# A two-layer network on one core: statistics' roots on VectorE, value maps ahead of the small maps, constants loaded over later slots

## The chip, the core and the metric

The kernel runs on one core of a Trainium2 chip. A core has five engines, each with its own queue of instructions: TensorE (PE in the profile, with its weight loads as PEld), VectorE (DVE), ScalarE (ACT), GpSimd (POOL) and SyncE (SP), which only issues transfers here. PSUM is the memory into which TensorE writes and from which VectorE and ScalarE read. Instructions of one engine run in their program order, and engines wait for each other through semaphores. The metric is the device time of one execution in microseconds (us); the time of the kernel before is the median of three runs.

## The reference, cut to what matters

The input x is 8 images of 256 channels by 64 by 64 pixels in float32. Two layers follow one another, each with a group norm ahead of it and a residual sum.

```python
x = x + L0(gn(x)); x = x + L1(gn(x))       # gn: 32 groups, (g - mean) / sqrt(var + 1e-5)

def L0(x):                                 # a conv whose weights are made from x
    x1, x2, x3 = conv1x1(x, w1, b1), conv1x1(x, w2, b2), conv1x1(x, w3, b3)   # 32, 32, 256 channels
    h = concat([x1, unfold3x3(reflect_pad(x2))])
    h = conv1x1(relu(bn1(h)), cw1)
    w = conv1x1(relu(bn2(h)), cw2, cb2)    # 9 weights for each of 32 groups
    return sum over the 9 taps of unfold3x3(pad(x3)) * w

def L1(x):
    q, k, v = three 1x1 convs of 256 channels, 4 heads
    att = softmax of q . (k + position) over a 7x7 window; out_att = att . v
    wts = softmax over 9 taps of conv1x1(x, Wfc)       # 9 x 256 channels
    oc = depthwise3x3(relu(depthwise3x3(x, w1_tap)), w2_tap), for each tap
    return rate1 * out_att + rate2 * sum over taps of oc * wts
```

`bn` is a batch norm with given statistics, which also takes `1 / sqrt(var + 1e-5)`.

## The kernel before

An image is cut into 8 bands of 8 rows (512 pixels), and the 256 channels into two halves of 128 partitions. Layer 0 runs 12 bands (`AHEAD`) ahead of layer 1. The outer loop counts g from -12 to 63: slots g < 0 hold layer 0 alone (the prologue, `alone` in the code); from g = 0 on, a slot holds band g of layer 1 and beside it band g + 12 of layer 0. A slot has 8 steps, each with six calls of `advance()`, so 48 to a slot. The order of the instructions is written out by hand: `beside(g, s)` gives what is issued in step s at its head, middle and end, and `after(n, f)` puts f behind the n-th `advance()` from now. Nothing reorders instructions afterwards; each engine gets its own in the order in which the program issues them.

Layer 0 of a band runs over three slots. In the first, `small_maps` makes x1 and x2 on TensorE (L328), and `write_maps` writes them with their bias by eight ScalarE instructions (L343) into three shifted copies; GpSimd fills the borders. `value_maps` makes x3 for each half (L369), ScalarE adds the bias (L374), and the result is stored to DRAM (L376), by ScalarE's queue in the prologue. In the prologue the small maps stand in step 0 and the value maps in steps 2 and 3; in the main loop the value maps stand at the end of step 0 and in step 1. In the second slot `hidden_maps` makes the hidden channels on ScalarE (L418) and TensorE (L428); `values_by_group` and `x_by_group` have SP load x3 and x in another layout (x3q, xg). In the third, `tap_weights` makes the nine weights on TensorE (pw, L464), VectorE multiplies them with the shifted values (prod, L477), and GpSimd adds six products into xg (L485). In the prologue the other three products are added up by TensorE (sco_sum, L498), VectorE combines both (L505), and `keep` stores the band by four transfers on ScalarE's queue (L523).

The group norm's statistics of an image are handled by `gn_affine`: group means by a small product pg (L237), their copies and differences gm and d (L246 to L250), a second product, then `sc = 1 / sqrt(pg + eps)` and `bi` (L269). Chain a (`scaled_weights`) belongs to layer 0 and goes on into scaled weights and a product pb (L304); chain b (`norm_rows`) belongs to layer 1 and goes on into a product pgc (L542). Chain a of image 0 stands ahead of all slots and that of image 1 in the prologue; those of images 2 to 7 lie in the main loop, in band 3 of an image. Chain b of images 1 to 7 lies in the main loop, in band 6. Their products take one of the four PSUM buffers of the tag "gen", which pq, pk, pf, pw, p3 and the transposed probabilities use too.

In layer 1 the scores (sco, L736) are the product of queries and kb, the keys with position, which VectorE finishes (L700, L707) right ahead of them. A score tile of two banks serves two steps. VectorE masks the scores and takes their minimum (L750), ScalarE takes the exponentials (L758), VectorE the reciprocal of their sums (L765), ScalarE scales (L767), TensorE transposes (ptp, L773), and the weighted values follow (small, L785). The branch of Wfc is the products pf (L872), ScalarE's exponentials (L877) and GpSimd's sums; VectorE runs the depthwise convolutions (acc, L829 and L855).

Of the kernel before, what the change touches and what calls it, by code (L numbers as in the profile page):

```python
# [9 lines left out]

F32 = mybir.dt.float32
BF16 = mybir.dt.bfloat16
AF = mybir.ActivationFunctionType
ALU = mybir.AluOpType
AX = mybir.AxisListType
# [3 lines left out]
P = 128  # L19
# [36 lines left out]
CHUNK = R * KW  # L56
NPROB = 2 * CHUNK
NEG = -1.0e30


AHEAD = NB + 4
# [25 lines left out]
def conv_layers_kernel(ctx: ExitStack, tc: tile.TileContext, ins: dict, out: bass.AP):  # L87
# [14 lines left out]
        return t  # L102


    late = []

    def load(name, shape, src=None, now=True):
        t = const.tile(shape, F32, name=f"c_{name}")
        late.append(lambda: nc.scalar.dma_start(out=t, in_=ins[name] if src is None else src))
        if now:  # L110
            late.pop()()
        return t

    gmat = load("gmat", [P, P])
# [13 lines left out]
    wfc = load("wfc", [P, NCT, KK - 1, C], wfc_in[:, :, : KK - 1], now=False)  # L128

    ident = const.tile([P, P], F32, name="ident")  # L130
    make_identity(nc, ident)
# [8 lines left out]
    for t in probs + x3n + h2n:  # L140
        nc.gpsimd.memset(t, 0.0)

    def rstd_(out_, var, eps):
        nc.vector.tensor_scalar(out_, var, eps, None, ALU.add)
        nc.scalar.activation(out_, out_, AF.Sqrt)
        nc.vector.reciprocal(out_, out_)


    bn1s = const.tile([P, 3], F32, name="bn1s")
    bn1b = const.tile([P, 3], F32, name="bn1b")  # L150
    bn2s = const.tile([P, 1], F32, name="bn2s")
    bn2b = const.tile([P, 1], F32, name="bn2b")
    for s, t, g, b_, m, v, n, p in (
        (bn1s, bn1b, PG, PB, PM, PV, 3, P),
        (bn2s, bn2b, PG2, PB2, PM2, PV2, 1, P),
    ):
        rstd_(s, par[:p, v : v + n], BN_EPS)
# [28 lines left out]
    def layer1_loads():  # L186


        last = w1.tile([P, NCT, 1, C], F32, tag="oc", name="last")
        for f in late:  # L190
            f()
        nc.scalar.dma_start(out=last, in_=wfc_in[:, :, KK - 1 :])

        def first():
            nc.vector.tensor_scalar(wv, wv, rate1, None, ALU.mult)

        def difference(kt):
            nc.vector.tensor_sub(wfc[:, kt], wfc[:, kt], last[:, kt].to_broadcast([P, KK - 1, C]))  # L200

        return [first, lambda: difference(0), lambda: difference(1)]

    class Image:
        def __init__(self):
# [9 lines left out]
    def after(n, f):  # L215
        later.append((place[0] + n, f))

    def advance():
# [3 lines left out]
        for f in ready:  # L222
            f()

    def gn_affine(sts, means, name, done):
# [7 lines left out]
        gm, d, sc, bi = (stat.tile([P, n], F32, name=f"{v}_{name}", tag=f"{v}{n}") for v in ("gm", "d", "sc", "bi"))  # L233

        def group_means(v, k):
            pg = ps.tile([P, n], F32, name=f"pg_{name}_{k}", tag="gen", bufs=4)
            nc.tensor.matmul(pg, means, v, start=True, stop=True)  # L237
            return pg


        def a1():
            pg = group_means(mean, 0)
            after(2, lambda: a2(pg))

        def a2(pg):
            nc.vector.tensor_copy(gm, pg)  # L246
            for ct in range(n):
                c = slice(ct, ct + 1)
                nc.vector.tensor_scalar(d[:, c], pg[:, c], mean[:, c], None, ALU.subtract)
                nc.vector.tensor_scalar(d[:, c], d[:, c], d[:, c], var[:, c], ALU.mult, ALU.add)  # L250
            after(5, a3)

        def a3():
            pg = group_means(d, 1)
            after(2, lambda: a4(pg))

        def a4(pg):
            nc.vector.tensor_scalar(sc, pg, GN_EPS, None, ALU.add)
            after(2, a5)

        def a5():
            nc.scalar.activation(sc, sc, AF.Sqrt)
            after(4, a6)

        def a6():
            nc.vector.reciprocal(sc, sc)
            for ct in range(n):
                c = slice(ct, ct + 1)
                nc.vector.tensor_scalar(bi[:, c], gm[:, c], sc[:, c], -1.0, ALU.mult, ALU.mult)  # L269
            done(sc, bi)  # L270

        after(3, a1)


# [13 lines left out]
    def scaled_weights(b):  # L288

        im = images[b]  # L290

        def scale(sc, bi):
            im.w12s = w0.tile([P, NCT, 2 * REL], F32, tag="w12s", name=f"w12s_{b}", bufs=1)
            im.w3s = w0.tile([P, NCT, C], F32, tag="w3s", name=f"w3s_{b}", bufs=1)
            for kt in range(NCT):
                nc.scalar.activation(im.w12s[:, kt], w12[:, kt], AF.Copy, scale=sc[:, kt : kt + 1])
                nc.scalar.activation(im.w3s[:, kt], w3[:, kt], AF.Copy, scale=sc[:, kt : kt + 1])
            after(5, lambda: through(bi))

        def through(bi):  # L300
            pb = ps.tile([P, 1 + NCT], F32, tag="gen", name=f"pb_{b}", bufs=4)
# [6 lines left out]
            after(2, lambda: biases(pb))  # L308
# [26 lines left out]
    def write_maps(b, i, p12):  # L335
        im = images[b]
        t = im.x2[i] = w0.tile([P, HR, W], F32, tag="x2", name=f"x2_{b}_{i}", bufs=2)
        bias = im.bias
        for u in range(2):
            r, o = u * R // 2, 64 * u  # L340
            for q, (dst, src) in enumerate(((1, 0), (0, 0), (0, 1))):
                n = W - (q != 1)
                nc.scalar.activation(  # L343
                    t[32 * q : 32 * q + 32, r + 1 : r + 1 + R // 2, dst : dst + n],
                    p12[o : o + 32, :, src : src + n], AF.Identity, bias=bias[o : o + 32, 0:1],
                )
            nc.scalar.activation(
                t[96:128, r : r + R // 2, :], p12[o + 32 : o + 64], AF.Identity, bias=bias[o + 32 : o + 64, 0:1]
            )
# [179 lines left out]
    def norm_rows(b):  # L529
        im = images[b]  # L530


        def keep(sc, bi):
            both = stat.tile([P, 2], F32, name=f"both_{b}", tag="both")
            nc.vector.tensor_copy(both[:, 0:1], sc)
            nc.vector.tensor_copy(both[:, 1:2], bi)
            after(3, lambda: by_channel(both))

        def by_channel(both):
            pg = ps.tile([P, NCT, 2], F32, tag="gen", name=f"pgc_{b}", bufs=4)  # L540
            for ct in range(NCT):
                nc.tensor.matmul(pg[:, ct], gc[:, ct], both, start=True, stop=True)  # L542
            after(2, lambda: take(pg))
# [369 lines left out]
    def beside(g, s):  # L913
# [48 lines left out]
        alone = g < 0  # L962
        if 0 <= g + AHEAD < B * NB:
            bq_, iq = divmod(g + AHEAD, NB)
            if alone and s == 0:
                mid.append(lambda: small_maps(bq_, iq, small_tile(f"{bq_}_{iq}"))())
            if s == (2 if alone else 0):
                (mid if alone else end).append(lambda: value_maps(bq_, iq, 0, alone))
            if s == (3 if alone else 1):
                mid.append(lambda: value_maps(bq_, iq, 1, alone))  # L970
        if 0 <= g + AHEAD - 1 < B * NB and s == (2 if alone else 1):
            bh, ih = divmod(g + AHEAD - 1, NB)
# [37 lines left out]
    with tc.manual_schedule():  # L1010
# [14 lines left out]
        scaled_weights(0)  # L1025
        for _ in range(32):
            advance()
        for n, f in enumerate(layer1_loads()):
            after(4 * STEPS * (3 + n), f)

        pending, before, conv, convs = [], None, None, []
        for g in range(-AHEAD, B * NB):
            b, i = divmod(g, NB)
            for s in range(STEPS):
# [156 lines left out]
```

## Time and profile before

| what | us |
|---|---|
| median of three runs (3908.52 to 3914.09) | 3910.43 |
| the profiled execution | 3911.49 |
| its span | 3909.7 |
| PE busy in it | 3778.1 |
| DVE, POOL, ACT busy | 3419.7, 3172.5, 2835.8 |
| first score matmul (end of the prologue) | 235.0 |
| first, second and third combination of a band (L505) | 68.86, 87.42, 103.78 |
| the two differences of Wfc on VectorE | start at 56.57 and 72.53 |
| issue and landing of the first x3q | 42.36, 50.22 |

The profile comes from one execution. Its span runs from the first to the last instruction; 1.8 us of the execution lie around it. Busy time of an engine counts the time in which it has an instruction under way; a share of 97% for PE is a mean over the prologue and the main loop. In a row of an engine's timeline the columns are the start, the duration, the engine, the line, the operation, and what it writes and reads; a bracket gives the idle time ahead of it and the engine and tile that ended it.

### The profile page before, as it was taken

What the parts mean: (1) busy time and instruction counts of PE and PEld (TensorE: products, weight loads), DVE (VectorE), ACT (ScalarE), POOL (GpSimd) and SP (SyncE); (2) the same over time, 40 slices, a digit from 0 to 9 for tenths busy, and PEclk for the clock granted to TensorE, in tenths of its full rate; (3) what the DMA queues carried; (4) which work ended last, traced back from release to release, by engine and by line L of the source; (5) the groups of instructions that cost most, each with busy time, mean ns of one, the idle gap of its engine ahead of it and who ended that gap; (6) DMA issues with size and microseconds to landing.
All of it is one profiled execution on the core that took longest, in us unless ns stands there. A gap on an engine that the chain in (4) does not pass through costs nothing.

```text
span 3909.7 us, 71679 instructions
## 1 busy us (share of the span) xinstructions
PE 3778.1 (97%) x24620; PEld 2112.2 (54%) x24620; DVE 3419.7 (87%) x7143; ACT 2835.8 (73%) x6779; POOL 3172.5 (81%) x2156
## 2 busy tenths in 40 slices
PE   5889999999999999999999999999999999999998
PEld 2445555555555555555555555555555555555554
DVE  6879898899898999899998998989988889978778
ACT  4457777777777777777777777777777777677776
POOL 4768888888887988888888888978988888956665
PEclk9999999999999999999999999999999999999999
DMA  8764443543444543543444443444433443322221
GB/s 245 208 168 128 127 118 115 143 121 116 124 123 123 142 118 105 140 131 114 139 111 128 136 119 113 127 138 116 130 111 100 133 122 94 87 85 79 72 60 35
DMA packets 429710, 473.36 MB, mean 121 GB/s; under 512 B 60992, under 2 KB 322208, under 8 KB 429088
## 3 DMA queue, kind: packets, MB, share of 16 engines
q1 hardware_dynamic: 412768, 453.01, 41.1%
q10 hardware_dynamic: 16576, 15.76, 1.3%
q8 instruction: 194, 3.18, 0.3%
q14 instruction: 172, 1.41, 0.1%
HBM read 329.08 MB, written 143.00 MB: 121 GB/s over the span
## 4 chain that ended last, share of the span: by engine, by line
PE 41%; DVE 24%; POOL 15%; ACT 11%; issue 6%; DMA 3%; SPq 0%; ACTq 0%; POOLq 0%; DVEq 0%
PE pf L872 19%; POOL xg L485 8%; DVE prod L477 7%; DVE acc L855 5%; DVE rec L893 5%; POOL ex L1087 4%; PE small L785 3%; PE pv L594 3%; ACT x L343 3%; PE ptp L773 3%; PE sco L736 3%; PE pk L692 2%; PE pq L670 2%; ACT ex L877 2%; DMA x<-x3n 2%
## 5 line engine op out<-in xcount | busy, mean ns | idle before, releaser
L872 PE MATMUL pf<-yp,c_wfc 128*128 128x512 f32 x4096 | 1916.6, 594 | 17.8 <-ACT ex L877 6.8
L485 POOL TENSOR_TENSOR xg<-xg,prod 128x1024 f32<-128x1024 f32 x549 | 1198.8, 2184 | 106.7 <-DVE prod L477 82.5
L872 PEld LDWEIGHTS pf<-yp,c_wfc 128*128 128x128 f32 x4096 | 738.5, 190 | 719.0 <-issue 629.2
L1087 POOL TENSOR_TENSOR ex<-ex,ex 128x1024 f32<-128x1024 f32 x384 | 908.2, 2365 | 66.4 <-ACT ex L877 62.5
L829 DVE SCALAR_TENSOR_TENSOR acc<-yp,c_chan,acc 128x504 f32<-128x504 f32 (+3 forms) x1104 | 775.4, 702 | 64.7 <-ACT acc L820 41.3
L477 DVE SCALAR_TENSOR_TENSOR prod<-pw,c_par,x3q 128x1040 f32<-128x1040 f32 x576 | 737.0, 1286 | 103.6 <-PE pw L464 57.4
L855 DVE SCALAR_TENSOR_TENSOR acc<-hid,c_chan,acc 128x504 f32<-128x504 f32 (+3 forms) x1024 | 750.6, 733 | 18.1
L877 ACT ACTIVATE ex<-pf 128x512 f32<-128x512 f32 x1024 | 602.0, 588 | 214.5 <-PE pf L872 197.5
L758 ACT ACTIVATE prob<-prob,nmax 128x196 f32<-128x196 f32 x1024 | 459.1, 451 | 224.5 <-DVE nmax L750 224.3
L767 ACT ACTIVATE prob<-prob,tot 128x196 f32<-128x196 f32 x1024 | 413.1, 452 | 249.5 <-DVE tot L765 248.3
L894 POOL TENSOR_TENSOR tot<-tot,rec 128x256 f32<-128x256 f32 x254 | 185.4, 730 | 398.0 <-DVE rec L893 391.6
L893 DVE RECIPROCAL rec<-tot 128x256 f32<-128x256 f32 x256 | 445.8, 1742 | 9.5 <-POOL tot L894 4.3
L775 ACT COPY pt<-ptp 112x512 f32<-112x512 f32 x511 | 295.0, 577 | 110.3 <-PE ptp L773 109.9
L750 DVE CUSTOM_DVE_ANT_0 prob<-sco,c_mask 128x196 f32<-128x196 f32 x1024 | 324.4, 354 | 28.1 <-PE sco L736 28.0
L773 PEld LDWEIGHTS ptp<-ident,prob 128*112 128x112 f32 x2044 | 227.2, 133 | 184.2 <-issue 157.1
L773 PE MATMUL ptp<-ident,prob 128*112 128x128 f32 x2044 | 319.0, 279 | 0.0
L785 PEld LDWEIGHTS small<-pt,vt 112*64 112x64 f32 x8144 | 258.2, 137 | 77.4 <-issue 75.7
L785 PE MATMUL small<-pt,vt 112*64 112x64 f32 x8144 | 293.7, 225 | 1.2 <-DMA vt<-vd 1.2
L369 PE MATMUL p<-xc,w3s 128*128 128x512 f32 x512 | 248.3, 608 | 15.8 <-ACT ex L877 15.8
L594 PE MATMUL pv<-c_wv,yp 128*128 128x256 f32 x1056 | 252.1, 381 | 7.4 <-ACT qb L674 6.0
L888 POOL TENSOR_SCALAR tot<-tot 128x512 f32<-128x512 f32 x127 | 243.6, 1918 | 11.1
L464 PEld LDWEIGHTS pw<-h2n,c_c 128*128 128x128 f32 x1152 | 176.2, 192 | 137.6 <-issue 122.7
(139 smaller groups left out, 4750.0 us busy)
## 6 DMA issues: line engine op xcount, KB each, us to landing
vt<-vd SPq DMA_DIRECT2D x512, 112.0 KB
x3q<-x SPq DMA_DIRECT2D x128, 264.0 KB
xc<-in_x SPq DMA_DIRECT2D x64, 512.0 KB
xg<-in_xg SPq DMA_DIRECT2D x64, 512.0 KB
yp<-x SPq DMA_DIRECT2D x128, 256.0 KB
xr<-x SPq DMA_DIRECT2D x64, 512.0 KB
out_x<-xr SPq DMA_DIRECT2D x64, 512.0 KB
xs<-in_x SPq DMA_DIRECT2D x57, 512.0 KB
```

Source lines behind the costliest of these rows:

```text
L477: nc.vector.scalar_tensor_tensor(prod[:, :, :RUN], pw[:, j, :RUN].unsqueeze(1).to_broadcast([P, SHARE, RUN]), par[:, PCB2 + k : PCB2 + k + 1],
L485: nc.gpsimd.tensor_add(im.xg[i], im.xg[i], rows(prod))
L758: nc.scalar.activation(prob[:, h, :NKEY], prob[:, h, :NKEY], AF.Exp, bias=nmax[:, h : h + 1], scale=-1.0, accum_out=tot[:, h : h + 1],)
L767: nc.scalar.activation(prob[:, h, :NKEY], prob[:, h, :NKEY], AF.Copy, scale=tot[:, h : h + 1])
L773: nc.tensor.transpose(ptp[:, h, ch], prob[:, h, ch * CHUNK : (ch + 1) * CHUNK], ident)
L785: nc.tensor.matmul(po[half[h], :, t * TQ : (t + 1) * TQ], im.vt[i + ch, m][:n, t, (2 * ct + h) * HD : (2 * ct + h + 1) * HD], pt[:n, h, ch ...
L829: nc.vector.scalar_tensor_tensor(o, yp[:, ct, ra + dr : rb + dr, ca + dc : cb + dc], chan[:, ct, CW1 + k : CW1 + k + 1], o, ALU.mult, ALU.add,
L855: nc.vector.scalar_tensor_tensor(o, hid[:, ra + dr : rb + dr, ca + dc : cb + dc], chan[:, ct, CW2 + k : CW2 + k + 1], o, ALU.mult, ALU.add,)
L872: nc.tensor.matmul(pf, wfc[:, kt, 2 * m + j, ct * P : (ct + 1) * P], images[b].yp[i][:, kt, PAD : PAD + R], start=(kt == 0), stop=(kt == N ...
L877: nc.scalar.activation(ex[:, j].rearrange("p (r c) -> p r c", r=R), pf, AF.Exp)
L893: nc.vector.reciprocal(rec, v)
L1087: after(4, lambda ex=ex, exb=exb: nc.gpsimd.tensor_add(ex, ex, exb))
```

## The change

Five things are changed.

- `rstd_`, which takes 1 / sqrt(var + eps), had a VectorE addition, a ScalarE square root and a VectorE reciprocal. It now has twelve VectorE instructions: an addition, a first guess from the bits of the number, and three Newton steps. It is used for the batch norms' constants and, in place of the three separate stages a4 to a6, in `gn_affine`. No square root is left on ScalarE.
- The distances of the chain are others: the reads of the small products one `advance()` behind them instead of two, the second product three behind the first one's reads instead of five, the product pgc five behind its input instead of three.
- In the main loop the products pg, pb and pgc go into columns of the current score tile which the scores don't use (`narrow`), no longer into a "gen" buffer.
- In the prologue the two value maps of a band are issued in step 0 and its small maps in step 1. The maps of the first two bands of image 0 are written by VectorE (`put`).
- The constants of layer 1 (Wq, Wk, Wv, Wfc, mask, the last tap of Wfc, about 3.3 MB) were all issued on ScalarE's queue ahead of the slots, with c2. Now c2 stays there; Wq and Wk are issued in slot 1, Wv and mask in 2, Wfc in four pieces in slots 3 to 6, the last tap in 5. The scaling of Wv by rate1 goes to slot 4 and the two differences of Wfc to slots 7 and 8.

```diff
-    def rstd_(out_, var, eps):
-        nc.vector.tensor_scalar(out_, var, eps, None, ALU.add)
-        nc.scalar.activation(out_, out_, AF.Sqrt)
-        nc.vector.reciprocal(out_, out_)
+    def rstd_(out_, var, eps, v, t):
+        bits = out_.bitcast(I32)
+        nc.vector.tensor_scalar(v, var, eps, None, ALU.add)
+        nc.vector.tensor_scalar(bits, v.bitcast(I32), 1, None, ALU.logical_shift_right)
+        nc.vector.tensor_scalar(bits, bits, -1.0, ROOT, ALU.mult, ALU.add)
+        for _ in range(3):
+            nc.vector.scalar_tensor_tensor(t, out_, -0.5, out_, ALU.mult, ALU.mult)
+            nc.vector.tensor_mul(t, t, v)
+            nc.vector.scalar_tensor_tensor(out_, t, 1.5, out_, ALU.add, ALU.mult)
...
-        return [first, lambda: difference(0), lambda: difference(1)]
+        late["c2"]()
+        return [
+            (1, late["wq"]), (1, late["wk"]), (2, late["wv"]), (2, late["mask"]),
+            (3, lambda: piece(0)), (4, lambda: piece(1)), (5, lambda: piece(2)), (6, lambda: piece(3)),
+            (5, lambda: nc.scalar.dma_start(out=last, in_=wfc_in[:, :, KK - 1 :])),
+            (4, scaled), (7, lambda: difference(0)), (8, lambda: difference(1)),
+        ]
...
+    def narrow(name, at, n):
+        if not beside_scores:
+            return ps.tile([P, n], F32, tag="gen", name=name, bufs=4)
+        return beside_scores[-1][:, 0, 2 * NKEY + at : 2 * NKEY + at + n]
...
         def group_means(v, k):
-            pg = ps.tile([P, n], F32, name=f"pg_{name}_{k}", tag="gen", bufs=4)
+            pg = narrow(f"pg_{name}_{k}", 4 * k, n)
...
         def a1():
             pg = group_means(mean, 0)
-            after(2, lambda: a2(pg))
+            after(1, lambda: a2(pg))
...
-            after(5, a3)
+            after(3, a3)
         def a3():
             pg = group_means(d, 1)
-            after(2, lambda: a4(pg))
+            after(1, lambda: a4(pg))
         def a4(pg):
-            nc.vector.tensor_scalar(sc, pg, GN_EPS, None, ALU.add)
-            after(2, a5)
-        def a5():
-            nc.scalar.activation(sc, sc, AF.Sqrt)
-            after(4, a6)
-        def a6():
-            nc.vector.reciprocal(sc, sc)
+            rstd_(sc, pg, GN_EPS, va, d)
...
+            if b == 0 and i < 2:
+                nc.vector.tensor_scalar(to, v, bias, None, ALU.add)
+            else:
+                nc.scalar.activation(to, v, AF.Identity, bias=bias)
...
-            after(3, lambda: by_channel(both))
+            after(5, lambda: by_channel(both))
...
-            if alone and s == 0:
+            if alone and s == 1:
                 mid.append(lambda: small_maps(bq_, iq, small_tile(f"{bq_}_{iq}"))())
-            if s == (2 if alone else 0):
+            if s == 0:
                 (mid if alone else end).append(lambda: value_maps(bq_, iq, 0, alone))
-            if s == (3 if alone else 1):
+            if s == (0 if alone else 1):
                 mid.append(lambda: value_maps(bq_, iq, 1, alone))
...
-        for n, f in enumerate(layer1_loads()):
-            after(4 * STEPS * (3 + n), f)
+        for n, f in layer1_loads():
+            after(6 * STEPS * n, f)
...
                         sco = score_tile(nm)
+                        beside_scores[:] = [sco]
```

More of the change, by code (lines that the diff above doesn't have):

```diff
@@ L11 @@
 F32 = mybir.dt.float32
-BF16 = mybir.dt.bfloat16
+I32 = mybir.dt.int32
 AF = mybir.ActivationFunctionType
@@ L58 @@
 NEG = -1.0e30
+ROOT = float(0x5F3759DF)
 AHEAD = NB + 4
@@ L102, in load_x @@
         return t
-    late = []
+    late = {}
     def load(name, shape, src=None, now=True):
         t = const.tile(shape, F32, name=f"c_{name}")
-        late.append(lambda: nc.scalar.dma_start(out=t, in_=ins[name] if src is None else src))
+        late[name] = lambda: nc.scalar.dma_start(out=t, in_=ins[name] if src is None else src)
         if now:
-            late.pop()()
+            late.pop(name)()
         return t
@@ L127, in conv_layers_kernel @@
     wfc_in = ins["wfc"].rearrange("(t p) k n -> p t k n", p=P)
-    wfc = load("wfc", [P, NCT, KK - 1, C], wfc_in[:, :, : KK - 1], now=False)
+    wfc = const.tile([P, NCT, KK - 1, C], F32, name="c_wfc")
     ident = const.tile([P, P], F32, name="ident")
@@ L141, in conv_layers_kernel @@
         nc.gpsimd.memset(t, 0.0)
-    def rstd_(out_, var, eps):
-        nc.vector.tensor_scalar(out_, var, eps, None, ALU.add)
-        nc.scalar.activation(out_, out_, AF.Sqrt)
-        nc.vector.reciprocal(out_, out_)
+    def rstd_(out_, var, eps, v, t):
[7 more added lines that the diff above has]
+            nc.vector.scalar_tensor_tensor(out_, t, 1.5, out_, ALU.add, ALU.mult)
+    root = [const.tile([P, 3], F32, name=f"root_{i}") for i in range(2)]
     bn1s = const.tile([P, 3], F32, name="bn1s")
@@ L156, in conv_layers_kernel @@
     ):
-        rstd_(s, par[:p, v : v + n], BN_EPS)
+        rstd_(s, par[:p, v : v + n], BN_EPS, root[0][:p, :n], root[1][:p, :n])
         nc.vector.tensor_mul(s, s, par[:p, g : g + n])
@@ L189, in layer1_loads, with piece, scaled @@
         last = w1.tile([P, NCT, 1, C], F32, tag="oc", name="last")
[L190 to L194, printed above, removed]
+        def piece(n):
+            kt, k = n // 2, slice(n % 2 * (KK // 2), (n % 2 + 1) * (KK // 2))
+            nc.scalar.dma_start(out=wfc[:, kt, k], in_=wfc_in[:, kt, k])
+        def scaled():
             nc.vector.tensor_scalar(wv, wv, rate1, None, ALU.mult)
@@ L223, in advance @@
             f()
+    beside_scores = []
+    def narrow(name, at, n):
+        if not beside_scores:
+            return ps.tile([P, n], F32, tag="gen", name=name, bufs=4)
+        return beside_scores[-1][:, 0, 2 * NKEY + at : 2 * NKEY + at + n]
     def gn_affine(sts, means, name, done):
@@ L232, in gn_affine @@
         mean, var = mv[:, :, 0], mv[:, :, 1]
-        gm, d, sc, bi = (stat.tile([P, n], F32, name=f"{v}_{name}", tag=f"{v}{n}") for v in ("gm", "d", "sc", "bi"))
+        gm, d, sc, bi, va = (stat.tile([P, n], F32, name=f"{v}_{name}", tag=f"{v}{n}") for v in ("gm", "d", "sc", "bi", "va"))
         def group_means(v, k):
-            pg = ps.tile([P, n], F32, name=f"pg_{name}_{k}", tag="gen", bufs=4)
+            pg = narrow(f"pg_{name}_{k}", 4 * k, n)
             nc.tensor.matmul(pg, means, v, start=True, stop=True)
@@ L300, in through @@
         def through(bi):
-            pb = ps.tile([P, 1 + NCT], F32, tag="gen", name=f"pb_{b}", bufs=4)
+            pb = narrow(f"pb_{b}", 8, 1 + NCT)
             for m, to, w in ((0, 0, w12), (0, 64, w12), (1, 0, w3[:, :, :P]), (2, 0, w3[:, :, P:])):
@@ L307, in through @@
                     )
-            after(2, lambda: biases(pb))
+            after(1, lambda: biases(pb))
         def biases(pb):
@@ L337, in write_maps, with put @@
         t = im.x2[i] = w0.tile([P, HR, W], F32, tag="x2", name=f"x2_{b}_{i}", bufs=2)
-        bias = im.bias
+        def put(to, v, o, n):
+            bias = im.bias[o : o + n, 0:1]
+            if b == 0 and i < 2:
+                nc.vector.tensor_scalar(to, v, bias, None, ALU.add)
+            else:
+                nc.scalar.activation(to, v, AF.Identity, bias=bias)
         for u in range(2):
@@ L342, in write_maps @@
                 n = W - (q != 1)
-                nc.scalar.activation(
+                put(
                     t[32 * q : 32 * q + 32, r + 1 : r + 1 + R // 2, dst : dst + n],
-                    p12[o : o + 32, :, src : src + n], AF.Identity, bias=bias[o : o + 32, 0:1],
+                    p12[o : o + 32, :, src : src + n], o, 32,
                 )
-            nc.scalar.activation(
-                t[96:128, r : r + R // 2, :], p12[o + 32 : o + 64], AF.Identity, bias=bias[o + 32 : o + 64, 0:1]
-            )
+            put(t[96:128, r : r + R // 2, :], p12[o + 32 : o + 64], o + 32, 32)
         nc.gpsimd.tensor_copy(t[0:32, 1 : 1 + R, 0:1], t[0:32, 1 : 1 + R, 2:3])
@@ L536, in keep @@
             nc.vector.tensor_copy(both[:, 1:2], bi)
-            after(3, lambda: by_channel(both))
+            after(5, lambda: by_channel(both))
         def by_channel(both):
-            pg = ps.tile([P, NCT, 2], F32, tag="gen", name=f"pgc_{b}", bufs=4)
+            pg = narrow(f"pgc_{b}", 12, NCT * 2).rearrange("p (t n) -> p t n", t=NCT)
             for ct in range(NCT):
                 nc.tensor.matmul(pg[:, ct], gc[:, ct], both, start=True, stop=True)
-            after(2, lambda: take(pg))
+            after(1, lambda: take(pg))
         def take(pg):
```

## The prediction

> **What bounds the kernel now.** I read the page's busy shares first, then the busy time by windows, then what TensorE (PE) waited for, then the timelines of PE and VectorE (DVE) at one statistics chain, and the chain of waits of one band of the prologue.
>
> ```profile
> PE 3778.1 (97%) x24620; PEld 2112.2 (54%) x24620; DVE 3419.7 (87%) x7143; ACT 2835.8 (73%) x6779; POOL 3172.5 (81%) x2156
> ```
> ```profile
> 0.00:60.00 60.00, 30.16 (x148) 15.86 (x150) 27.89 (x59) 23.88 (x46) 12.35 (x28) 0.94 0.80 265
> ...
> 120.00:235.00 115.00, 95.39 (x455) 50.49 (x453) 92.31 (x114) 50.65 (x93) 91.56 (x67) 0.90 0.73 203
> ...
> 1000.00:2000.00 1000.00, 983.75 (x6508) 553.98 (x6507) 899.31 (x1887) 751.65 (x1801) 859.49 (x580) 1.00 0.44 124
> ```
>
> PE is busy 98.4% of the main loop, but half of the first 60 us and 83% of the later prologue, at a granted clock of 0.90. So there are two cases: a prologue of 235 us (first score matmul at 235.0) that is a chain of dependent work, and a main loop in which only a PE gap costs time. The most that the main loop can give is its gaps:
>
> ```profile
> PE p L369 <- ACT ex L877: 13.8, 51, 0.5
> ...
> PE sco L736 <- DVE kb L707: 5.2, 29, 0.2
> PE pg_a L237 <- ACT ex L877: 5.0, 6, 0.8
> PE pg_b L237 <- ACT ex L877: 2.3, 6, 0.4
> ```
>
> The chains' own gaps are the last two rows, 7.3 us, and about 0.75 us of pf once per image behind the b chain's table load (at 632.25, 1103.31 and so on). The row of kb matters more: the score matmul waits for VectorE's key products by 0.2 us at most, 29 times, so these two arrive together. Anything that holds VectorE ahead of kb goes straight to PE. One a chain, VectorE first:
>
> ```profile
> 439.65 0.27 DVE L250 TENSOR_SCALAR d_a<-d_a,mv_a 128x1 f32<-128x1 f32 x1
> 439.84 1.29 DVE L477 SCALAR_TENSOR_TENSOR prod<-pw,c_par,x3q 128x1040 f32<-128x1040 f32 x1
> ...
> 442.82 1.52 DVE L855 SCALAR_TENSOR_TENSOR acc<-hid,c_chan,acc 128x504 f32<-128x504 f32 x2
> 444.25 0.16 DVE L765 RECIPROCAL tot<-tot 128x2 f32<-128x2 f32 x1
> 444.33 0.73 DVE L700 SCALAR_TENSOR_TENSOR kb<-pk,c_chan,pe 128x512 f32<-128x512 f32 x1
> 444.98 0.52 DVE L707 SCALAR_TENSOR_TENSOR kb<-pk,c_chan,pe 128x16 f32<-128x16 f32 x3
> ```
> ```profile
> 438.10 1.88 PE L872 MATMUL pf<-yp,c_wfc 128*128 128x512 f32 x4
> ...
> 442.97 0.38 PE L237 MATMUL pg_a<-d_a,c_gmat 128*128 128x2 f32 x2 [0.84 <-ACT ex L877]
> ...
> 445.65 0.92 PE L736 MATMUL sco<-kb,qb 64*64 64x196 f32 x16
> ```
>
> VectorE has no gap from 434 on, kb ends at 445.50, the scores start at 445.65.
>
> **Main loop, chain a (six times: images 2 to 7).** The built order of instructions moves two things. PE's second product pg_a stands 2 steps earlier, behind pw_1 and ahead of pf, ptp and pk. VectorE's twelve-instruction root and the two bi stand ahead of L765's reciprocal and of kb; before, one short L258 stood behind kb. (1) PE reaches the product at 438.10, and d_a ends at 439.65 + 0.27 = 439.92: a wait of 1.8 us where 0.84 was; pf, ptp and pk behind it move by 1.0. (2) VectorE's root would begin at 444.25. Its instructions each read the one before; starts of such dependent pairs stand 0.25 (438.97 to 439.22, L249 to L250) and 0.19 us (L250 to L249) apart. Twelve at 0.2 make 2.4, two bi (0.21 each, L269) 0.35: kb ends at 445.50 + 2.75 = 448.25. The score matmul waits for it, and behind it stand small, ptp and the next pf, while ScalarE's exponentials wait for the scores: +2.75 of PE's time, the 1.0 of (1) being inside it. By pitches of 0.12 (the tightest pair, L535 to L536) it is +1.8, by 0.27 (L250's whole duration) +3.6. I take 2.75, as the shapes are L249's and L250's: 6 x 2.75 = 16.5.
>
> **Chain b (seven times: images 1 to 7).** Same picture at 606 to 640: the product is reached at 613.85 and its d_b ends at 615.26; kb ends at 620.84 and the scores start at 620.99. Root, bi and two copies ahead of kb: 2.4 + 0.2 + 0.3 = 2.9, of which 0.2 is slack: +2.7. The 0.75 gap of pf behind the table load goes: +1.95, times 7 = 13.7. A table load costs ScalarE 1.28 us (L262: 13 loads, 16.7 us, and as many back at L877); ScalarE is busy 75% here, so beyond the gaps named their going is worth nothing. Together 30.2; some later gaps (13.8 us of p behind ex) should close when PE comes later, for which I take off 2: +28. Ends: +14 with the short pitch and gaps closing, +38 with the long one.
>
> [...]
>
> **Small products beside the scores.** Four PSUM buffers are spared and nothing in the rows of before waits for one; the score tile must now be read by VectorE before it is reused. Those reads stand early (gm, d) or in the block priced above: 0; if the root's first read came late, its tile is reused two score tiles on, so the wait would be that of kb again.
>
> **Prologue, the steady band.** One band takes 16.36 us (the combining products, L505, at 87.42, 103.78, 120.15). Chain of waits of before:
>
> ```profile
> 97.86 1.01 PE small L328 x8
> 98.88 0.87 PE pw L464 x6
> 99.75 1.79 PE sco_sum L498 x4
> 101.54 1.73 PE p L369 x4
> ...
> 110.31 0.81 ACT hid L418
> ```
>
> The value map p is on it once, small once, and ScalarE's eight write_maps (8 x 0.460, L343, 3.7 us) are not: they run beside pw, sco_sum and p. In the new order both value maps come first (2 x 1.73), then pw, sco_sum, small, and the eight writes come only then, ahead of hid on ScalarE. So the cycle is hid and ph 1.28, pw 0.87, sco_sum 1.72, value maps 3.44, pw 0.87, sco_sum 1.8, small 1.02, writes with their issue 4.0, two hid 1.42, four issues of L523 2.65 = 19.1: +2.7 a band. Full price falls on the four bands combined at 103 to 160 less what they wait already: I take +2.7 for three, +1 at the image change (22 us there, with slack), and +2.2, +1.9, +1.5 for the last ones, together +14.7.
>
> **Prologue, the start.** The constants' root on VectorE (24 short instructions among the statistics) and that of GN (12) put the biases about 3 us later (25.2 to 28.3). VectorE writes the maps of bands 0 and 1 (16 at 0.31, an estimate from 0.354 for 128x196, L750, and 0.66 for 128x512, L700): 5.0 us against 7.4 on ScalarE. Behind them in VectorE's order stand the statistics of the next tile, on which SP's load of xs_2 waits, and behind that on SP's queue xg_0 and x3q_0: x3q_0 is issued at 46.9 or later, where it was 42.36. First combination: +2.7. In its favour, about 3.3 MB of constants leave the first 60 us, where the DMA share is 0.80: x3q_0 took 7.9 us from issue to landing. The Wfc differences leave bands 0 and 1 (4.20 and 2.28 us of VectorE at 56.57 and 72.53) for slots 7 and 8, where VectorE has room (17 of 22 us): -0.9 to -3.4. The nine moved issues cost ScalarE 0.33 to 0.56 each (L376, L523) in either place: 0. Start together: -0.7, between -8 (x3q without queueing) and +6. Prologue: +14, ends -8 and +25.
>
> [...]
>
> **Sum.** 3911.5 (profiled execution: span 3909.7 and 1.8 around it) + 28 + 14 = 3953.5; it stands 1.1 above the median, so 3952.
>
> **Rivals.**
> - Faster, by VectorE's queue at the chains: it comes to the root early, because PE's longer wait at the product also holds back the pw and pf whose products VectorE would otherwise do first, so kb is no later and all the chains' gaps go: 7.3 + 7 x 0.75 = 12.6. With a prologue in the middle between its -8 and the cycle's cost (0) that is 3898. For it: the root asks VectorE for 2.4 us in a band of 57.6 of which it is busy 90%; against: no gap on VectorE from 434, no slack at kb. It decides from a root block under 0.7 us ahead of kb.
> - Prologue gains, chains pay: the start is limited by DMA (share 0.80), x3q_0 lands up to 8 us earlier and the band keeps 16.4, ScalarE's writes lying beside the longer PE run: -8 + 28: 3930. Against it: the writes wait for a small map that PE does last.
> - Colder prologue: 1.7 on nine bands beside the +42: 3967. For it: 3.58 for four sco_sum in slots that wait 2 us; against: 1.96 after as long a gap.
> - Chains lose their gaps while the prologue pays, 14 - 12.6: 3912, no change.
>
> **Chances.** Forecast 0.37, faster 0.23, prologue gains 0.19, colder 0.13, no change 0.08. A measurement of this kernel tells 0.2% (8 us) from no change. Faster 0.23, same 0.08, slower 0.69. Likeliest case's own range 3938 to 3966; the range that takes in the others is 3899 to 3970.
>
> **What would show it.** Right: PE gaps of 1.8 us at the second pg_a and 2 to 3 us ahead of sco with releaser kb, once per chain, the root's instructions starting 0.2 us apart; L505 spaced 19 us in bands 2 to 4; first score matmul at 245 to 253. Wrong if kb still ends with the scores' start in the bands of the chains, if L505 stays at 16.4, or if the first combination comes ahead of 66.

## The result and the profile after

The changed kernel takes 4048.98 us (median of four runs, 4045.73 to 4049.72) where the kernel before took 3911.4 in the same session: slower by a ratio of 1.0351, 95% interval 1.0335 to 1.0367. That is 138 us more, where the forecast was 3952 us, some 42 more. The profiled execution has a span of 4047.9 us, 138.2 more than before.

The first part of the page of the changed kernel, the busy time of each engine, and from what TensorE waited for (columns: who waited for whom, us in total, times, longest) the rows that are new:

```profile
PE 3829.4 (95%) x24620; PEld 2141.5 (53%) x24620; DVE 3514.7 (87%) x7339; ACT 2807.5 (69%) x6718; POOL 3174.5 (78%) x2156
```
```profile
PE sco L753 <- DVE kb L724: 40.9, 41, 4.5
PE sco L257 <- DVE nmax L767: 40.8, 13, 3.5
```

PE is busy 51 us longer although it issues the same number of matmuls, so some of them ran slower; the other 87 of the 138 us are idle time. The row of kb, which was 5.2 us with 0.2 at the longest, is now 40.9 with 4.5. The second row did not exist: 13 times a product of the chains (L257 now writes into a score tile, so the trace names its output sco) waits for VectorE's masks. Thirteen is the number of chains in the main loop.

Where the time went, by the starts of the first score matmul of each band: band 0 starts at 274.6 instead of 235.0 (+39.6), and its own time falls from 64.7 to 59.1 (-5.6). Band 3 of images 0 to 5, with chain a, goes from 60.4 to 67.5 once and 68.9 five times: together +50.0. Band 6, with chain b, goes from 57.8 to 65.8 or 66.3 in images 0 to 5 and from 48.1 to 51.8 in image 6: +52.6. All other bands are within 0.1. The sum of these is 136.6 of 138.2.

One chain a in the changed kernel, VectorE's timeline:

```profile
473.71 0.27 DVE L270 TENSOR_SCALAR d_a<-d_a,mv_a 128x1 f32<-128x1 f32 x1
...
475.67 0.09 DVE L767 DVE_READ_ACCUMULATOR2_ANT nmax<- 128x1 f32 x1
...
478.50 0.67 DVE L148 TENSOR_SCALAR sc_a<-va_a 128x2 int32<-128x2 int32 x1
479.20 0.17 DVE L149 TENSOR_SCALAR sc_a<-sc_a 128x2 int32<-128x2 int32 x1
479.41 2.03 DVE L151 SCALAR_TENSOR_TENSOR d_a<-sc_a 128x2 f32<-128x2 f32 x1
481.47 2.27 DVE L152 TENSOR_TENSOR d_a<-d_a,va_a 128x2 f32<-128x2 f32 x1
483.77 0.16 DVE L153 SCALAR_TENSOR_TENSOR sc_a<-d_a,sc_a 128x2 f32<-128x2 f32 x1
...
486.11 0.53 DVE L724 SCALAR_TENSOR_TENSOR kb<-pk,c_chan,pe 128x16 f32<-128x16 f32 x3
```

GpSimd's at the same time:

```profile
476.98 4.43 POOL L502 TENSOR_TENSOR xg<-xg,prod 128x1024 f32<-128x1024 f32 x2
481.38 2.33 POOL L1105 TENSOR_TENSOR ex<-ex,ex 128x1024 f32<-128x1024 f32 x1
489.43 2.20 POOL L502 TENSOR_TENSOR xg<-xg,prod 128x1024 f32<-128x1024 f32 x1 [5.72 <-DVE prod L494]
```

Three of the root's instructions, on two numbers per partition, last 0.67, 2.03 and 2.27 us. L148 comes once in a root; L151 and L152 come twice more, and last 0.16 each time. The ends of the long ones are 479.17, 481.44 and 483.74; GpSimd's three sums end at 479.14 (the first of the two in the row of 476.98), 481.41 and 483.71. From then on GpSimd is idle until 489.43 and nothing is long. Each of the three lasts until the GpSimd instruction under way is over. The block from L147 (478.31) to the start of the reciprocal of L782 (485.39) takes 7.08 us, and kb ends at 486.64.

And TensorE's, with its granted clock (PEclk, the third number from the right) in the three stretches before, between and after:

```profile
471.70 0.61 PE L481 MATMUL pw<-h2n,c_c 128*128 128x132 f32 x4
475.81 0.59 PE L257 MATMUL sco<-d_a,c_gmat 128*128 128x2 f32 x2 [3.49 <-DVE nmax L767]
476.25 3.76 PE L889 MATMUL pf<-yp,c_wfc 128*128 128x512 f32 x4
...
480.66 2.62 PE L709 MATMUL pk<-yp,c_wk 128*128 128x512 f32 x4
...
486.78 0.92 PE L753 MATMUL sco<-kb,qb 64*64 64x196 f32 x16 [1.34 <-DVE kb L724]
```
```profile
469.90:475.80 5.90, 2.42 (x11) 1.26 (x9) 5.79 (x16) 3.90 (x7) 5.74 (x6) 0.96 0.00 0
475.80:483.10 7.30, 7.29 (x14) 3.72 (x15) 7.13 (x8) 1.89 (x6) 7.22 (x4) 0.57 0.71 238
483.10:490.00 6.90, 5.56 (x81) 3.66 (x79) 6.58 (x23) 4.06 (x11) 1.18 (x2) 1.00 1.03 211
```

The input d_a of the second product is there at 473.98, but the product starts at 475.81, just behind the last read of the masks (475.67 + 0.09): the masks read the score tile into which it writes. Behind this gap of 3.49 us the granted clock is 0.57, and four pf take 3.76 us instead of 1.88. PE so loses 3.5 us by the wait and 3.1 by the slower clock ahead of the scores, and still comes 1.34 us earlier than kb. This is the first chain of the main loop and the one with the longest stretch at the slower clock: in the other eleven of bands 3 and 6 the wait for the masks is 3.0 to 3.5 us too, the slower clock costs 1.7 us in nine and nothing in two, and kb comes 2.8 to 4.5 us behind PE.

### The profile page after: what moved, and what is told of

It reads as the page before. It is cut to its first block, busy times and chain, and to the rows that moved or that the text cites. A ratio compares the mean times of both kernels' runs of the same rounds, so it can differ in the third digit from the quotient of the medians.

```text
span 4047.9 us, 71784 instructions
## 1 busy us (share of the span) xinstructions
PE 3829.4 (95%) x24620; PEld 2141.5 (53%) x24620; DVE 3514.7 (87%) x7339; ACT 2807.5 (69%) x6718; POOL 3174.5 (78%) x2156
## 4 chain that ended last, share of the span: by engine, by line
PE 44%; DVE 28%; POOL 11%; ACT 9%; issue 5%; DMA 2%; ACTq 0%; SPq 0%; POOLq 0%; DVEq 0%
PE pf L889 21%; DVE prod L494 7%; POOL xg L502 6%; DVE acc L872 6%; DVE rec L910 5%; PE small L802 4%; ACT x L356 4%; PE pv L611 4%; PE ptp L790 3%; PE sco L753 3%; PE pk L709 3%; PE pq L687 3%; POOL ex L1105 2%; DVE acc L846 2%; DVE prob L767 2%
## 5 line engine op out<-in xcount | busy, mean ns | idle before, releaser
L846 DVE SCALAR_TENSOR_TENSOR acc<-yp,c_chan,acc 128x504 f32<-128x504 f32 (+3 forms) x1104 | 775.4, 702 | 67.6 <-ACT acc L837 47.2
L802 PEld LDWEIGHTS small<-pt,vt 112*64 112x64 f32 x8144 | 266.6, 141 | 77.9 <-issue 77.6
L802 PE MATMUL small<-pt,vt 112*64 112x64 f32 x8144 | 302.3, 229 | 0.0
L753 PE MATMUL sco<-kb,qb 64*64 64x196 f32 x4096 | 238.4, 346 | 44.0 <-DVE kb L724 40.9
```

Source lines behind the costliest of these rows:

```text
L802: nc.tensor.matmul(po[half[h], :, t * TQ : (t + 1) * TQ], im.vt[i + ch, m][:n, t, (2 * ct + h) * HD : (2 * ct + h + 1) * HD], pt[:n, h, ch ...
L846: nc.vector.scalar_tensor_tensor(o, yp[:, ct, ra + dr : rb + dr, ca + dc : cb + dc], chan[:, ct, CW1 + k : CW1 + k + 1], o, ALU.mult, ALU.add,
```

## The experiments

Each kernel is the changed one with one part undone or altered, but for split_root and ln_exp, which start from the kernel before. Times are of one run each, except the last two and the changed kernel; the kernel before had 3909 to 3915 beside them. "Product" is the start of the first of VectorE's products in the prologue, "combined" that of the first combination, "band 0" that of its first score matmul (all in us from the span's start); bands 3 and 6 are lengths in the middle images. A version with the root's scratch in PSUM (own_psum) has no measured time.

| kernel | time | product | combined | band 0 | band 3 | band 6 |
|---|---|---|---|---|---|---|
| before | 3910.4 | 50.2 | 68.9 | 235.0 | 60.4 | 57.8 |
| changed | 4049.0 | 60.4 | 79.3 | 274.6 | 68.9 | 65.8-66.3 |
| own_buffer | 4055.6 | 57.9 | 74.8 | 272.4 | 68.9-69.4 | 66.1-66.5 |
| sqrt_back | 4016.7 | 59.0 | 77.8 | 267.3 | 66.7-68.4 | 63.1 |
| root_columns | 4008.1 | 62.2 | 79.1 | 275.4 | 67.5-68.2 | 60.3 |
| sqrt_own | 3958.5 | 55.8 | 74.7 | 264.4 | 62.4 | 58.9 |
| chains_back | 3936.3 | 57.4 | 74.3 | 263.2 | 60.4 | 57.9 |
| order_only | 4050.8 | 59.6 | 81.5 | 276.5 | 68.9 | 65.8-66.3 |
| order_back | 4032.2 | 54.2 | 70.8 | 251.0 | 68.9 | 66.3 |
| writes_back | 4048.1 | 55.8 | 76.1 | 269.4 | 68.9 | 65.8-66.3 |
| loads_only_late | 4033.6 | 52.3 | 70.5 | 250.4 | 68.9 | 65.8-66.3 |
| first_back | 4026.2 | 52.8 | 70.0 | 242.3 | 68.9 | 65.8-66.3 |
| split_root | 3959.7 | 48.2 | 67.7 | 237.6 | 65.2-68.2 | 59.2-60.8 |
| ln_exp | 3919.8 | 50.9 | 70.2 | 240.7 | 61.4 | 57.9 |

**The chains: own_buffer.**

```diff
-        if not beside_scores:
+        if True:
             return ps.tile([P, n], F32, tag="gen", name=name, bufs=4)
```

> The small products of the chains go back to buffers of their own; the root stays on VectorE with its scratch in SBUF. Theory 'held root' (three of the root's twelve instructions each wait until the GpSimd instruction under way has ended, so kb comes 7.1 us late): band 3 keeps 67 to 69 us (60.4 before, 68.9 after), band 6 some 65 (57.8 before, 65.8 after), though the wait of 3.5 us at the second product goes. Theory 'product behind the mask' (the second product waits for the masks that VectorE reads from the same score tile, and TensorE runs at half clock after that gap): band 3 falls to 63 or less, and the whole by 13 x 5 = 65 us.

Bands 3 and 6 stay at 69 and 66. TensorE's timeline of two chains a in this kernel, and its row of kb among the waits:

```profile
485.82 1.59 PE L753 MATMUL sco<-kb,qb 64*64 64x196 f32 x16 [5.57 <-DVE kb L724]
...
966.33 0.35 PE L257 MATMUL pg_a<-d_a,c_gmat 128*128 128x2 f32 x2 [1.80 <-DVE d_a L270]
966.54 3.66 PE L889 MATMUL pf<-yp,c_wfc 128*128 128x512 f32 x4
...
978.99 0.92 PE L753 MATMUL sco<-kb,qb 64*64 64x196 f32 x16 [3.89 <-DVE kb L724]
```
```profile
PE sco L753 <- DVE kb L724: 72.1, 42, 5.7
```

The product no longer waits for the masks, 1.80 us are left for d_a, and what PE gains there it spends waiting for kb: 72.1 us in all instead of 40.9, and 5.6 in five of the six chains a. The chain shown at 966 is the exception: behind the same 1.80 us its four pf take 3.66, where they take 1.96 in the other five. The root's block alone costs as much as the whole.

A band can also lose by the clock alone. Band 3 of image 0 lasts 73.5 us here, where it was 67.5 in the changed kernel: behind the wait of 5.57 us the granted clock is 0.50 from 485.8 to 496, although PE is busy without a gap.

**sqrt_back.** In `gn_affine` the call of the new root gives way to the three stages of before (`add`; two `advance()` later `AF.Sqrt`; four later `reciprocal`); the products stay beside the scores.

> The chains take ScalarE's square root and VectorE's reciprocal again, the small products stay beside the scores. 'Held root': kb is on time again, and what is left is the product behind the mask: 3.5 us of wait plus 3 us of half clock less the 0.84 of before, band 3 at about 66. If the wait at the product is covered by slack, band 3 is at 60 to 62.

Band 3 is at 66.7 to 68.4 and band 6 at 63.1. TensorE in chain a:

```profile
953.66 0.38 PE L257 MATMUL sco<-d_a,c_gmat 128*128 128x2 f32 x2 [3.48 <-DVE nmax L775]
953.90 2.90 PE L897 MATMUL pf<-yp,c_wfc 128*128 128x512 f32 x4
...
961.80 0.92 PE L761 MATMUL sco<-kb,qb 64*64 64x196 f32 x16
...
972.59 1.39 PE L324 MATMUL sco<-bi_a,c_w 128*64 128x1 f32 x16 [2.01 <-DVE nmax L775]
```

The score matmul waits for nothing (no bracket), but the second product has waited 3.48 us for the masks, with four pf behind it that take 2.90 us instead of 1.96, and the product pb waits 2.01 us for the next masks. So the place of the products costs something by itself too. Against sqrt_own (below), which differs in nothing but this place, it is 4.3 to 6.0 us in band 3 and 4.2 in band 6; the root by itself, own_buffer against sqrt_own, costs 6.5 to 7.6. The two losses lie over each other: both together cost no more than the root alone.

**root_columns.** Buffers of their own as in own_buffer, and the root written so that no instruction reads two tiles of SBUF or works on more than one element per partition:

```diff
-            rstd_(sc, pg, GN_EPS, va, d)
+            by_columns(sc, pg, GN_EPS, va, d, n)
...
+        for c in (slice(k, k + 1) for k in range(n)):
+            y, vc, tc_ = out_[:, c], v[:, c], t[:, c]
...
+            for _ in range(3):
+                nc.vector.tensor_scalar(tc_, y, y, -0.5, ALU.mult, ALU.mult)
+                nc.vector.tensor_scalar(tc_, tc_, vc, 1.5, ALU.mult, ALU.add)
+                nc.vector.tensor_scalar(y, y, tc_, None, ALU.mult)
```

> Products in buffers of their own as in own_buffer, and the root is done one column at a time by instructions that read one tile of SBUF and take the other factor as a per-partition scalar, like L270's (0.27 us, never longer): 12 of them in chain b, 24 in chain a. 'Held root': no instruction is held, b's block takes 2.5 to 3.2 us in place of 6.9 and band 6 falls from 66.1 to about 60.5; a's block takes 5 to 6 us in place of 7.1, band 3 at 66 to 68. Rival 'short dependent instructions are slow beside GpSimd whatever they read': some still last 2 us and band 6 stays at 66.

Band 6 falls to 60.3; band 3, with 24 instructions, only to 67.5 to 68.2. The groups of VectorE's lines, first of the changed kernel, then of this one (after the bar: busy us, mean ns of one, idle before):

```profile
L151 DVE SCALAR_TENSOR_TENSOR d_b<-sc_b 128x1 f32<-128x1 f32 x24 | 21.9, 912 | 0.8
```
```profile
L253 DVE TENSOR_SCALAR d_b<-sc_b 128x1 f32<-128x1 f32 x24 | 5.1, 214 | 0.8
```

The mean of 912 ns is a mix of 0.16, 0.7 to 1.5 and 2.3 us; the same step in the other form takes 214 ns, and in the trace no instruction of the new root, of which 239 of 288 started while GpSimd was at work, lasts over 0.22 us. Twelve dependent short instructions are not slow in themselves; what held them was the GpSimd instruction beside them.

**sqrt_own and chains_back.** The first undoes root and place together; the second restores the distances too (2, 5, 2 and 3 `advance()`, as before).

> Both parts of the chains undone at once: ScalarE's square root, and buffers of their own; the shorter distances and the new prologue stay. If the held root and the product behind the mask are the two causes, each of which alone costs most of the loss, bands 3 and 6 come back to 60 to 62 and 58 to 59, and the whole falls to about 3950. If either distance or another part costs, they stay above 63 and 60.

> The chains wholly as before: ScalarE's square root, buffers of their own, the longer distances. The new prologue stays. If root, product and distances are all that the chains lost, bands 3 and 6 are at 60.4 and 57.8 to 58.0 again, where sqrt_own, with the short distances, left 62.4 and 58.9; what remains above the kernel before is the prologue alone, about 25 to 30 us.

With sqrt_own band 3 is at 62.4, a little above what was expected, and band 6 at 58.9: the shorter distances cost 2.0 and 1.0 by themselves, since the product is issued ahead of its input (PE waits 1.80 us for d_a in chain a, 1.35 for d_b in chain b). With chains_back they are at 60.4 and 57.9. The main loop's loss is thereby wholly found, and the remaining 27 us (3936.3 against 3909.0, one run against a median) are the prologue.

**The prologue: first_back, order_back, loads_only_late, order_only, writes_back.** All have the changed chains. The order of the slots is put back by

```diff
-            if alone and s == 1:
+            if alone and s == 0:
...
-            if s == 0:
+            if s == (2 if alone else 0):
...
-            if s == (0 if alone else 1):
+            if s == (3 if alone else 1):
```

VectorE's writes by making `if b == 0 and i < 2` false, and the loads by issuing all of them in `layer1_loads` with the three VectorE steps where they were.

> The slots ahead of band 0 as before: small maps first, value maps in steps 2 and 3, all maps written by ScalarE, layer 1's constants loaded at the start; the chains as in the changed kernel. If the prologue's loss is these three, the first score matmul comes back from 274.6 to 235 to 240 us and the whole falls by 30 to 35. If the roots of the batch norms and of the first images' chains on VectorE carry part of it, it stays above 242.

> Only the order of the prologue's slots as before (small maps in step 0, value maps in steps 2 and 3); the late loads and VectorE's writes stay, the chains as changed. If the order lengthens each band by 2.7 us, as the prediction had it, the combinations come back to 16.4 apart and band 0 from 274.6 to about 250. If the start (first product at 60.4 against 50.2) is what costs, band 0 gains less than 15.

> Order of the prologue and ScalarE's writes as before, only the loads of layer 1's constants stay late. Against first_back, where all three were undone and band 0 stood at 242.3: if the loads at the start crowd the DMA queues, band 0 comes at 232 to 240; if the loads in the slots collide with the bands' own transfers, it comes at 245 or later.

> Of the three changes to the prologue only the order of its slots stays (value maps first); loads at the start and ScalarE's writes as before, chains as changed. Against first_back (band 0 at 242.3): if the order costs by itself what it costs on top of the late loads and VectorE's writes (274.6 - 251.0 = 23.6), band 0 comes at 264 to 268. If it costs through VectorE's writes alone (the small maps, done later, hold them and SP's queue behind them), band 0 comes ahead of 255.

> Of the changed kernel only VectorE's writes of the first two bands' maps go back to ScalarE. If they hold back the start (SP's load of the next tile waits for statistics that stand behind them on VectorE), the first product comes 3 us or more ahead of 60.4 and band 0 ahead of 271. If the order alone sets the start, both stay within 1.5 us.

Band 0 starts at 242.3 with all three back; at 250.4 with late loads alone, 251.0 with late loads and VectorE's writes, 276.5 with the order alone, 269.4 with order and late loads, 274.6 with all three. By the start of band 0 the order costs 34 us by itself (276.5 against 242.3), 24 with late loads and VectorE's writes (274.6 against 251.0) and 19 with late loads (269.4 against 250.4). A part of it comes back at once: band 0 itself lasts 59 us with the new order and 64 to 66 with the old one, so that by the start of band 1 these are 28, 19 and 13. VectorE's writes cost 1 to 5 by the start of band 0, and late loads cost 8 with the old order and gain 7 with the new one.

The expectations fared as follows. first_back stays above 242, and falls by 23 us where 30 to 35 were expected. In order_back band 0 comes at 251.0, as expected, but the combinations stand 18.6, 17.8, 17.2 and 20.2 apart, not 16.4. loads_only_late comes later than 245, though by another cause than the one that was named, as seen below. writes_back gains what was expected at both places, and yet its time is that of the changed kernel, since band 3 of image 0 lasts 73.5 us instead of 67.5 (granted clock 0.53 from 480 to 490). Neither expectation of order_only held; its band 0 is the latest of all.

Two causes are seen in order_only. The combinations stand 20.3, 19.5, 18.6 and 20.1 apart, where first_back has 18.6, 16.4, 16.4 and 17.1: 2.5 us more a band. And the first combination comes 11.5 us later. ScalarE's timeline in order_only:

```profile
35.71 0.34 ACTq L391 DMA_DIRECT2D x<-x3n  x1
36.09 3.83 ACT L354 ACTIVATE x<-small,bias 32x252 f32<-32x252 f32 x8 [0.42 <-PE small L338]
43.37 0.69 ACT L389 ACTIVATE x3n<-p,bias 128x512 f32<-128x512 f32 x1 [3.45 <-DMA x<-x3n]
...
44.76 0.69 ACT L389 ACTIVATE x3n<-p,bias 128x512 f32<-128x512 f32 x1 [0.70 <-DMA x<-x3n]
```

The value maps of band 1 need x3n back from the two stores of band 0. These go out behind 3 MB of constants; the second, issued at 35.71, lands at 44.7 (the chain of waits has 8.97 us for it). ScalarE stands still for them, with band 1's writes and both hidden maps queued behind. With VectorE's writes and late loads (the changed kernel) the first store, issued at 33.77, holds ScalarE until 35.84 and the second, issued at 36.56, does not hold it at 38.72; but another queue stands still, SP's:

```profile
36.80 0.37 SPq L100 DMA_DIRECT2D xc<-in_x  x1
47.32 0.37 SPq L100 DMA_DIRECT2D xs<-in_x  x1
47.74 0.46 SPq L422 DMA_DIRECT2D xg<-in_xg  x1
48.30 6.82 SPq L407 DMA_DIRECT2D x3q<-x  x4
55.61 0.54 SPq L415 DMA_DIRECT2D x3q<-x  x1
```

SP issues nothing between 36.8 and 47.3 because the load of xs waits for the statistics that VectorE makes behind the sixteen writes (L354, 36.81 to 45.98 with the wait for the second small map between them). The DMA share is 0.00 from 43.0 to 47.3, and then xs, xg, Wv, mask and x3q come at once (share 1.05 from 48.0 to 60.2): x3q_0 is landed at 60.23. In order_back, with the small maps first, the same load of xs is issued at 41.57 and the first product starts at 54.19.

Most of what late loads cost with the old order, 6.9 of 8.1 us, is the two differences of Wfc. VectorE in loads_only_late, in the band in which the next image's statistics are due:

```profile
136.72 3.36 DVE L206 TENSOR_TENSOR c_wfc<-c_wfc,last 128x2048 f32<-128x2048 f32 x1
140.00 1.29 DVE L494 SCALAR_TENSOR_TENSOR prod<-pw,c_par,x3q 128x1040 f32<-128x1040 f32 x1
141.22 1.27 DVE L295 BATCH_NORM_STATS2 st<-xs 128x6 f32<-128x512 f32 x2
142.41 1.28 DVE L494 SCALAR_TENSOR_TENSOR prod<-pw,c_par,x3q 128x1040 f32<-128x1040 f32 x1
143.61 0.58 DVE L251 BATCH_NORM_AGGREGATE mv_a<-st 128x2 f32<-128x48 f32 x2
144.12 1.15 DVE L522 TENSOR_TENSOR xg<-sco_sum,xg 128x1024 f32<-128x1024 f32 x1
```

It starts while a GpSimd sum (135.74 to 137.93) is under way, lasts 3.36 us instead of the 2.28 that it takes in first_back, and everything down to the combination at 144.12 follows without a gap. Against first_back the combinations fall back by 3.6 us here and by 3.3 at the second difference.

**Versions meant to beat both: split_root and ln_exp.** The first takes the root of root_columns into the chains of the kernel before, in four parts two `advance()` apart and behind kb. The second replaces the square root and the reciprocal:

```diff
-            nc.scalar.activation(sc, sc, AF.Sqrt)
+            nc.scalar.activation(sc, sc, AF.Ln)
+            nc.scalar.activation(sc, sc, AF.Exp, scale=-0.5)
...
-            nc.vector.reciprocal(sc, sc)
```

> The kernel before, with only the chains of the main loop changed: the root one column at a time as in root_columns, no instruction of which was held, in four parts two steps apart and none of them ahead of kb in the step of the second product; buffers, distances and prologue as before. If the place and the holding made the root costly, bands 3 and 6 stay at 60.4 and 57.8 or fall by up to 0.8 (the gaps behind ScalarE's table loads), and the whole is 0 to 8 us faster than before. If VectorE has no room for the root, the bands grow by 1 us or more, the whole by 13.

> The kernel before; in the chains, ScalarE's square root and VectorE's reciprocal give way to ScalarE's Ln and Exp(-0.5 x), nothing is added on VectorE, and buffers, distances and prologue stay. If one set of tables serves Ln and Exp, the 26 table loads of 1.28 us go; the gap of 0.75 us behind b's load goes once per image and the whole falls by 4 to 8 us. If the tables are still switched, or the gaps close only to open elsewhere, the whole stays within 0.1% of 3909.

Both take longer than the kernel before, split_root by a ratio of 1.0126 (1.0109 to 1.0143) and ln_exp by 1.0021 (1.0012 to 1.0030), so split_root loses some 50 us where 13 were expected at worst, and ln_exp fits neither of its expectations. In split_root no root instruction is long and kb is on time, but the parts lie ahead of the masks of the next step. ScalarE and TensorE in one chain b:

```profile
641.05 0.46 ACT L782 ACTIVATE prob<-prob,nmax 128x196 f32<-128x196 f32 x1 [2.98 <-DVE nmax L774]
```
```profile
642.58 1.98 PE L896 MATMUL pf<-yp,c_wfc 128*128 128x512 f32 x4 [2.37 <-ACT ex L901]
```

ScalarE's queue stands at the exponential that needs nmax; the exponential that frees the buffer of pf is behind it, and PE waits 2.37 us for that (2.98 in chain a). VectorE had no room in these steps either; other places were not tried. In ln_exp the tables are still switched, now twice per chain and both times ahead of the next work of ScalarE; its band 3 is 1.0 us longer and its band 0 starts 5.7 later:

```profile
L262 ACT ACT_TABLE_LOAD x16 | 20.5, 1283 | 0.3
L263 ACT ACT_TABLE_LOAD x16 | 20.5, 1283 | 0.3
```

## Why the prediction was wrong

The direction and most of the places were right: slower, at chains a and b and in the prologue, with kb as the releaser of the score matmul. The sum was too small: it had +28 us for the main loop, which lost 102.6, and +14 for the prologue, which lost 34.0 by the start of band 1. These terms failed:

- **"Twelve at 0.2 make 2.4".** The place was right (kb waits for the root, PE for kb), and so is 2.4, nearly, for instructions that nothing holds: in root_columns chain b's twelve take 2.8 us (661.46 to 664.26), and band 6 is up 2.5 where the prediction had 1.95 a chain. In the changed kernel root and bi take 6.8, since three instructions are held beside GpSimd for 0.5, 1.9 and 2.1 us. The pitch was taken from L249 and L250, which in 39 starts beside a working GpSimd were never held; they work on one element and read one tile of SBUF at most besides a per-partition scalar. The rows of before had a hint, which the prediction names without asking for the cause: of two equal Wfc differences one took 4.20 us and one 2.28. In the trace of the changed kernel all 32 instructions of L151, L152 and L153 that started beside a working GpSimd, each with two inputs in SBUF, ended within 0.03 us after GpSimd's, while the depthwise sums of L846, which read one tile in SBUF and one in PSUM (acc), started beside it 870 times and never lasted over 0.76 us. L148 reads one tile, and its six starts on two elements beside GpSimd were held too, until 0.03 us after its end at most, and lasted 0.67 to 0.69 us. Why the one form is held and the other is not, no run shows.
- **"Small products beside the scores: 0".** This step failed in its mechanism. The product was priced with a wait for d_a of 1.8 us, which is what own_buffer shows (1.80). Beside the scores it waits for the masks that read the same tile: 3.0 to 3.5, and in sqrt_back pb and pgc wait 2.0 again for the next masks.
- **The half clock in the main loop was left out.** A slower TensorE was a rival for the prologue alone. In the first chain the granted clock is 0.50 from 475.8 to 482.1. Of the 8.6 us that band 3 of image 1 grew by, 5.4 are idle time and 3.2 slower matmuls. Behind gaps of 3.0 to 3.5 us four pf take 2.5 to 3.8 us in ten of the twelve chains in bands 3 and 6 of the changed kernel, and 1.96 in two. Behind the 1.80 of chains a in own_buffer they take 3.66 in one of six and 1.96 in the rest. The length of the gap alone does not tell which: behind two gaps of 3.03 us in the changed kernel, ahead of the chains b at 2610 and 3099, four pf take 1.96 and 2.46.
- **The start, "-0.7, between -8 and +6".** The first combination came 10.4 later. That SP's queue would stand behind VectorE's writes was foreseen (issue of x3q_0 "at 46.9 or later", measured 48.30), but the sixteen writes took 0.48 each, not 0.31, and the transfers held back then went out together with x3q_0, which took 11.9 us to land instead of 7.9.
- **The Wfc differences, "-0.9 to -3.4".** In the old order late loads cost 8.1. A mean of 17 busy us in 22 said that VectorE had room; the row just ahead of the statistics of the next image had none.
- **The bands of the prologue, "together +14.7".** "+2.7 a band" was right for one band (2.5 in order_only), but from the first combination to the first score matmul it is 195.3 us instead of 166.2, so +29.2. The order alone, order_only against first_back, makes 22.6 of it: the last two steps before band 0 cost 3.8 and 4.6 where the prediction had 1.9 and 1.5, and why is not shown.

Of the rivals, "faster by VectorE's queue" fell: VectorE never comes early. "Colder prologue" has some truth, the granted clock in 120 to 180 us being 0.80 where it was 0.89 before. Its 1.7 us in each of nine bands no run shows: of the 27 groups of four sco_sum in the prologue 11 take 2.95 to 3.78 us, where 6 took 2.97 to 3.76 before, and the others 1.88 to 1.99; all 27 take 69.7 us instead of 61.2. What stays open: first_back still starts band 0 at 242.3, 7.3 us behind the kernel before. Its trace points to the roots in the chains of images 0 and 1. The lag is 1.1 us at the first combination, grows by 2.3 at the one behind chain a of image 1, where L149 lasts 2.04 us, and by 3.2 at the one behind chain b of image 0, where L151 lasts 1.92. Going back to the square root in the chains alone (sqrt_back) also moves band 0 by 7.3; both undone together was not tried.

## What to carry to other kernels

Price a new VectorE instruction by rows of its own form (how many SBUF tiles it reads, how many elements) that ran beside a busy GpSimd: here a two-element multiplication cost 2.27 us, as much as the GpSimd sum beside it, and the form that reads one tile and a per-partition scalar, on one element, took 0.21. A small result put into free columns of another's PSUM tile inherited here the wait for that tile's readers, 3.0 to 3.5 us. In a bound loop ask for each queue which instruction stands at its head when the new one is late: here the score matmul, the masks and the exponentials each passed 2 to 4 us on to TensorE, and a gap of 3 us mostly cost 1.7 more in clock.

## What the runs showed of the hardware that was not expected

- The same instruction was held on two elements per partition and not on one: L148, the bit shift, lasted up to 0.69 us and L149 up to 2.03 on two; on one, in chains b, each started eight times beside a working GpSimd and never lasted over 0.16.
- Behind gaps of 1.80 us TensorE mostly kept its pace: four pf took over 2.8 us behind it in one of six chains a in each of own_buffer, root_columns and sqrt_own, and 1.96 in the others; after 1.35 in chains b of these runs they took 1.96 every time.
- In ln_exp each Ln and each Exp behind it came with a table load of 1.28 us: 32 loads in 16 chains.
